# Layer 0's down projection by seven block products from the second chunk on, its right operands prepared in the first

## The chip, the cores and the metric

The kernel runs on one core of one Trainium2 chip. A core has a matrix engine (TensorE, PE in the profile; its weight loads are PEld), three engines for elementwise work (VectorE or DVE, ScalarE or ACT, GpSimd or POOL) and a queue engine (SyncE, SP). Each takes its own instructions strictly in the order in which the built program holds them, and semaphores make one wait for another. DMA transfers are issued by SP, ACT and POOL. The metric is the device time of one execution in microseconds (us), lower is better.

## What is computed

Two layers over 4 sequences of 512 tokens, 512 wide, in float32. Layer 0 adds to its input a recurrent attention and a feed-forward block (FFN), both on the same normed input; layer 1 does the same with latent attention and an expert FFN. The change touches layer 0 alone. Its parts, cut from the reference:

```python
# recurrence of the attention, over 32 mini-batches of K = 16 tokens, 32 heads of 16
def step(carry, x):
    W1_s, b1_s = carry
    xq, xk, xv, eta_mb = x
    Z1 = xk @ W1_s + b1_s
    grad = _ln_fused_l2_bwd(Z1, xv - xk, ln_w, ln_b)
    Attn1 = jnp.tril(xq @ xk.swapaxes(-1, -2))
    b1_bar = b1_s - jnp.tril(eta_mb) @ grad
    Z1_bar = xq @ W1_s - eta_mb * Attn1 @ grad + b1_bar
    last_eta = eta_mb[:, :, -1, :, None]
    W1_new = W1_s - (last_eta * xk).swapaxes(-1, -2) @ grad
    b1_new = b1_s - jnp.sum(last_eta * grad, axis=-2, keepdims=True)
    out = xq + _ln(Z1_bar, ln_w, ln_b)
    return ((W1_new, b1_new), out)

# FFN, 512 -> 1408 -> 512
g = jnp.einsum('th,ih->ti', xf, gate_w) * gate_s
u = jnp.einsum('th,ih->ti', xf, up_w) * up_s
hdn = jax.nn.silu(g) * u
out = jnp.einsum('ti,hi->th', hdn, down_w) * down_s

x = x + _L0_attn_ref(xn, ...) + _L0_ffn_ref(xn, ...)
```

## The kernel before

Layer 0 takes about the first 975 us. Its 2048 tokens are handled in 8 chunks (`NCHUNK`) of 256: 4 sequences of 64 tokens. A chunk holds 4 steps of the recurrence (`CH`), so there are 32 steps (`NM`).

The recurrence is a chain of small operations over several engines. The main loop (L781 to L797) does for each step `n`: `weights_out` copies the state `wacc` into the block-diagonal operand `wq_bd`; `first_product` (PE) forms `pz`; `queries_out` (PE) begins `pso`; `gradient` is some fifteen short operations on DVE and ACT from `pz` to `grad`; `out_operands` builds `gh` on POOL; `update` (L393) copies `grad` into `g_bd` and adds to `wacc` on PE, with `km` from POOL as the other operand; `emit_out` (L434) finishes `pso` on PE from `gh`; `prepare` (L303) fetches the next step's `kv` on POOL's queue and makes `sk` and `km` on POOL.

While the chain runs over DVE, ACT and POOL, PE does other work. That work is a generator, `work` (L698), which chains `between(ch)` over the chunks, and `fill(us)` takes pieces from it until their declared PE times (the numbers that they `yield`) add up to `us`. The tuple `GAPS` (L37) gives the filler between a step's parts: before the update, before the output, after it; `LAST_GAPS` does so for the last chunk's steps. `between(ch)` (L656) consists of: 11 times `gate_up` (two products of 128x256 over 4 blocks each, then SiLU and a product into `hid`), the constants of the end (`finish_constants`, chunk 0 alone), then, interleaved by `take`, the next chunk's transposes, keys, token tiles and queries (`nxt`), `down`, and pieces of `finish(ch - 1)`, which normalises the attention's output, multiplies it by `wo`, adds the FFN's part `yf` and writes the layer's result.

The program is then built by a scheduler that sets each engine's order of instructions itself, from its own estimates of when operands are ready and from the order of the code. So what stands between two of a step's parts on PE in the built program is not what `GAPS` names, only near it.

`down(ch, u)` (L483) computes 128 rows of the FFN's output: for each of 11 blocks `i` of 128 inner columns it loads 256 KB of `in_wd` on SP's queue into a tile `w` (tag `wd`, 4 buffers) and multiplies `hid` by it into `pd`, 512 columns wide. Then DVE multiplies by the row `dsc` (`down_s` spread over all partitions), and POOL adds `brow` (a constant row from the post-norm's bias) and the residual `xr`, which it loads itself.

A tile pool hands out buffers in rotation per tag: a tile asked for under a tag waits until the tile that held its buffer has had its last reader. Loads stand in their queue's order, so one that waits for a buffer holds up those behind it.

Four-byte matmuls are recorded twice each in the profile (a program's matmul of `pd` counts 2 in the table).

Of the kernel before, what the change touches and what calls it, by code (L numbers as in the profile page):

```python
# [12 lines left out]
F32 = mybir.dt.float32  # L13
# [5 lines left out]
P = 128  # L19
B, L, HS = 4, 512, 512  # L20
# [3 lines left out]
NH, HD, K = 32, 16, 16  # L24
# [7 lines left out]
CW = B * CT  # L32
NS = 8
RW = 2 * 64 + 4

START = 20.0
GAPS, LAST_GAPS = (11.0, 3.0, 8.0), (10.0, 3.0, 7.0)  # L37
LAST_FINISH = (10.0, 14.0, 7.0, 0.0, 3.0, 1.0)
TTT_EPS = 1e-6
LN_EPS = 1e-5  # L40
# [2 lines left out]
NI = INTER // P  # L43
# [12 lines left out]
def trunk_kernel(ctx: ExitStack, tc: tile.TileContext, a: dict, out: bass.AP):  # L56
    nc = tc.nc
# [8 lines left out]
    ident = const.tile([P, P], F32, tag="ident", name="ident")  # L66
# [39 lines left out]
    with ExitStack() as px:  # L106
# [9 lines left out]
        def mm(out, lhsT, rhs, start=True, stop=True):  # L116
            nc.tensor.matmul(out, lhsT=lhsT, rhs=rhs, start=start, stop=stop, skip_group_check=True)  # L117

        def psum():
            return ps_pj.tile([P, 512], F32, tag="pj", name="pj")  # L120
# [61 lines left out]
        nc.scalar.dma_start(out=rows_small[:, P:], in_=a["tok"].unsqueeze(0))  # L182
        bones = load(one, "bones", [P, P], eng=nc.scalar)
        m2 = load(one, "m2", [P, 2], eng=nc.scalar)
        gamma_row = wk.tile([P, HS], F32, tag="xr", name="gamma_row")
        gbeta_row = one.tile([P, HS], F32, tag="gbeta_row", name="gbeta_row")
        lrw = load(one, "lrw", [P, NC, P], a["lrw"].rearrange("(c p) m -> p c m", p=P))
        wq_w = load(one, "wq", [P, NC, HS], a["wq"].rearrange("(c p) o -> p c o", p=P))
# [12 lines left out]
        tok = lrb[:, P:]  # L201


        sel8 = one.tile([NS, P], F32, tag="sel8", name="sel8")
        tok8 = one.tile([NS, 2, 4, HD], F32, tag="tok8", name="tok8")
        for h in range(2):
            r = slice(4 * h, 4 * h + 4)
            nc.gpsimd.dma_start(
# [249 lines left out]

        gs = load(one, "gs", [P, NI], eng=nc.gpsimd)
        us = load(one, "us", [P, NI], eng=nc.gpsimd)  # L460
        dsc = one.tile([P, HS], F32, tag="dsc", name="dsc")
        nc.gpsimd.dma_start(out=row["dsc"], in_=a["dsc"].unsqueeze(0))
        hid, yf = {}, {}

# [36 lines left out]
        ch8 = one.tile([NS, 4, 32], F32, tag="ch8", name="ch8")  # L501
# [12 lines left out]

        def finish_constants():
            nc.sync.dma_start(out=wo, in_=a["wo"].rearrange("(c p) o -> p c o", p=P))
            spread_row(dsc, row["dsc"])
            pt = psum()[:, :NS]
            nc.tensor.transpose(pt, ch8.rearrange("s al x -> s (al x)"), ident[:NS, :NS])
            nc.vector.tensor_copy(by_ch, pt)  # L520
            yield 1.0

            pt = psum()[:, :NC]
            mm(pt, onesd, beta_ch)
            beta_m = wk.tile([P, 1], F32, tag="beta_m", name="beta_m", bufs=1)
            nc.vector.tensor_reduce(beta_m, pt, AX.X, ALU.add)
            nc.vector.tensor_scalar(beta_ch, beta_ch, beta_m, None, ALU.subtract)

            pr = psum()
            for c in range(NC):  # L530
                pnb_b = wk.tile([P, P], F32, tag="pnb_b", name=f"pnb_b{c}")
# [190 lines left out]
        pt = psum()[:, :P]  # L722
# [186 lines left out]
    with ExitStack() as px:  # L909
# [623 lines left out]
```

## Time and profile before

| | |
|---|---|
| runs | 1992.97, 1993.64, 1996.19 us; median 1993.64 |
| profiled execution | 1996.04 us, span 1994.3 us |
| mean granted PE clock | 0.994 |
| PE busy | 1938.3 us, 97% |
| DVE, ACT, POOL busy | 1169.6 (59%), 816.1 (41%), 528.2 (26%) us |
| matmuls of the way down, `pd` | 352 records, 166.1 us |
| matmuls of `gate_up`, `pf` | 1408 records, 343.2 us |
| loads of `in_wd` | 176 of 256 KB, 3.1 us from issue to landing |

The span is what the profiler saw of one execution; about 1.7 us of the execution lie around it. "Busy" is the union of an engine's instruction times. Matmuls overlap one another in the pipeline, so the mean time of one record (600 ns for `pd`) is longer than the distance from one to the next.

```profile
PE   8999999999999999998999999999999999999999
DVE  4445748466666657474555656556555655655565
POOL 5333343424333342512000101111211121222223
DMA  6757566646456455745651135444344444333344
```

This is the span in 40 slices of some 50 us, each digit a share of busy time in tenths. Layer 0 fills the first 20: there DVE, POOL and the DMA engines are at work beside PE throughout, and PE has its few gaps.

### The profile page before, as it was taken

How to read it: one execution, taken by the hardware profiler on the slowest of the kernel's cores; microseconds unless marked ns; L12 is line 12 of the kernel's file. 1: busy time of each engine (PE TensorE's matmuls, PEld its weight loads, DVE VectorE, ACT ScalarE, POOL GpSimd, SP SyncE). 2: the span in 40 equal slices, each digit the busy share in tenths (PEclk: the TensorE clock that was granted, in tenths of full speed). 3: DMA queues.
4: the chain of work that ended last, by engine and by line, in shares of the span. 5: the costliest groups of instructions: out<-in, count | busy, mean ns of one | idle time of the engine just before them, and what ended most of it. 6: DMA issues, size and time to landing. Idle time of an engine off the chain costs nothing.

```text
span 1994.3 us, 32414 instructions
## 1 busy us (share of the span) xinstructions
PE 1938.3 (97%) x11626; PEld 1233.3 (62%) x11626; DVE 1169.6 (59%) x2579; ACT 816.1 (41%) x1695; POOL 528.2 (26%) x643
## 2 busy tenths in 40 slices
PE   8999999999999999998999999999999999999999
PEld 6777676767766676753777744555555555555555
DVE  4445748466666657474555656556555655655565
ACT  2234333334433443422222155455545545555552
POOL 5333343424333342512000101111211121222223
PEclk9999999999999999999999999999999999999999
DMA  6757566646456455745651135444344444333344
GB/s 170 210 130 209 143 185 167 175 120 179 141 145 189 126 173 159 224 128 195 225 168 49 58 94 141 118 106 104 101 111 108 103 110 108 95 101 98 89 115 117
DMA packets 226924, 273.51 MB, mean 137 GB/s; under 512 B 88587, under 2 KB 117452, under 8 KB 226124
## 3 DMA queue, kind: packets, MB, share of 16 engines
q1 hardware_dynamic: 204928, 237.19, 43.3%
q0 software_dynamic: 9760, 28.41, 5.0%
q10 hardware_dynamic: 12076, 5.84, 1.0%
q8 instruction: 93, 1.52, 0.3%
q14 instruction: 67, 0.55, 0.1%
HBM read 174.18 MB, written 34.87 MB: 105 GB/s over the span
## 4 chain that ended last, share of the span: by engine, by line
PE 49%; DVE 1%; DMA 0%; ACT 0%; issue 0%; SPq 0%; DVEq 0%; ACTq 0%
PE pc L1254 11%; PE sc L1207 9%; PE pq L1184 8%; PE px L1301 5%; PE p L1301 4%; PE pk L1184 3%; PE epg L976 3%; PE epo L1039 1%; PE epu L976 1%; PE eox L1069 1%; PE pvo L891 1%; PE pw L866 1%; PE eo L1069 1%; DMA gu<-in_gu 0%; DVE st L1225 0%; ACT prob L1227 0%
## 5 line engine op out<-in xcount | busy, mean ns | idle before, releaser
L1225 DVE TENSOR_REDUCE st<-sc 128x1 f32<-128x512 f32 x256 | 168.9, 681 | 244.0 <-PE sc L1207 244.0
L1227 ACT ACTIVATE prob<-sc,st 128x512 f32<-128x512 f32 x256 | 175.1, 686 | 210.5 <-DVE st L1225 210.3
L1254 PE MATMUL pc<-prT,lv 128*128 128x512 f32 x512 | 230.8, 593 | 0.0
L1232 ACT ACTIVATE prob<-prob,st 128x512 f32<-128x512 f32 x256 | 181.9, 720 | 58.8 <-DVE st L1231 58.8
L1236 DVE STREAM_TRANSPOSE tt<-prob 128x512 f32<-128x512 f32 x256 | 178.4, 700 | 43.0 <-ACT prob L1232 36.5
L117 PE MATMUL pf<-xT,wg 128*128 128x256 f32 x704 | 175.6, 391 | 6.2 <-DMA wg<-in_wg 4.4
L1184 PE MATMUL pq<-cq,uq 128*128 128x512 f32 x384 | 175.2, 592 | 0.0
L117 PE MATMUL pf<-xT,wu 128*128 128x256 f32 x704 | 167.6, 381 | 1.5 <-DMA wu<-in_wu 1.5
L117 PE MATMUL pd<-wd,hid 128*128 128x512 f32 x352 | 166.1, 600 | 1.3 <-DMA wd<-in_wd 1.2
L1254 PEld LDWEIGHTS pc<-prT,lv 128*128 128x128 f32 x512 | 96.4, 190 | 100.1 <-issue 98.1
L117 PEld LDWEIGHTS pf<-xT,wg 128*128 128x128 f32 x704 | 133.2, 194 | 33.5 <-issue 4.7
L1207 PE MATMUL sc<-k,q 32*128 32x512 f32 x1024 | 145.7, 617 | 2.5 <-ACT prob L1227 2.5
L117 PEld LDWEIGHTS pf<-xT,wu 128*128 128x128 f32 x704 | 134.5, 191 | 20.5 <-DMA wu<-in_wu 1.9
L478 DVE SCALAR_TENSOR_TENSOR hid<-pf,us,sg 128x256 f32<-128x256 f32 x88 | 42.0, 478 | 156.9 <-ACT sg L477 156.4
L1184 PEld LDWEIGHTS pq<-cq,uq 128*128 128x128 f32 x384 | 74.1, 193 | 90.7 <-issue 90.0
L314 POOL TENSOR_SCALAR sk<-k,m 128x256 f32<-128x256 f32 x64 | 61.2, 968 | 179.9 <-PE pz L117 167.7
L1195 POOL TENSOR_TENSOR kr<-kr,t2k 128x512 f32<-128x512 f32 x16 | 20.3, 1270 | 332.3 <-DVE t2k L1194 332.3
L421 POOL TENSOR_SCALAR gh<-grad,m 128x256 f32<-128x256 f32 x64 | 61.2, 966 | 154.5 <-DVE grad L390 131.6
L117 PEld LDWEIGHTS pd<-wd,hid 128*128 128x128 f32 x352 | 63.4, 190 | 60.2 <-issue 43.8
L1207 PEld LDWEIGHTS sc<-k,q 32*128 32x128 f32 x1024 | 48.4, 185 | 82.7 <-issue 73.2
L477 ACT ACTIVATE sg<-pf,gs 128x256 f32<-128x256 f32 x88 | 41.6, 473 | 132.8 <-PE pf L117 132.3
L1256 ACT COPY ctxT<-pc 128x512 f32<-128x512 f32 x64 | 37.4, 585 | 127.2 <-PE pc L1254 127.1
(316 smaller groups left out, 3467.9 us busy)
## 6 DMA issues: line engine op xcount, KB each, us to landing
prT<-tt SPq DMA_DIRECT2D x992, 64.0 KB, 2.0
wd<-in_wd SPq DMA_DIRECT2D x176, 256.0 KB, 3.1
wg<-in_wg SPq DMA_DIRECT2D x88, 256.0 KB, 3.0
wu<-in_wu SPq DMA_DIRECT2D x88, 256.0 KB, 3.1
cq<-lat_d SPq DMA_DIRECT2D x48, 256.0 KB, 3.8
rows<-rows SPq DMA_DIRECT2D x128, 66.0 KB, 2.2
kv<-rows POOLq DMA_DIRECT2D x32, 264.0 KB, 4.1
gu<-in_gu SPq DMA_DIRECT2D x3, 2048.0 KB
```

What stands on the lines that cost most here:

```text
L117: nc.tensor.matmul(out, lhsT=lhsT, rhs=rhs, start=start, stop=stop, skip_group_check=True)
L314: nc.gpsimd.tensor_scalar_mul(sk[:, :, :, h, :], at(k1[ch], slice(0, P)), m2[:, h : h + 1])
L421: nc.gpsimd.tensor_scalar_mul(gh[:, :, h, :], g, m2[:, h : h + 1])
L976: nc.tensor.matmul(ps, lhsT=w[:, c, :], rhs=x[:, c], start=start and c == 0, stop=c == 1, skip_group_check=True)
L1184: nc.tensor.matmul(ps, lhsT=columns(ws[hg][w]), rhs=x, start=(i == 0), stop=(i == len(srcs) - 1))
L1207: nc.tensor.matmul(ps[h], lhsT=qk[f"q{c}"][r, i * P : (i + 1) * P], rhs=qk[f"k{c}"][r, :], start=(n == 0), stop=(n == 2),)
L1225: pin(nc.vector.tensor_reduce(mx, ps[h], AX.X, ALU.max, negate=True))
L1227: pin(nc.scalar.activation(pr, ps[h], AF.Exp, bias=mx, scale=1.0, accum_out=sm))
L1232: pin(nc.scalar.mul(pr, pr, sm))
L1236: nc.vector.transpose(out=tt[:, :, h - 2], in_=pr.rearrange("p (k kq j) -> p kq k j", kq=4, j=32))
L1254: pin(nc.tensor.matmul(pc, lhsT=lv[:, b, k, :], rhs=at[:, :, k, :], start=(k == 0), stop=(k == E - 1)))
L1301: nc.tensor.matmul(ps[:, q, :], lhsT=a[:, k, q * P : (q + 1) * P], rhs=w[:, k, :], start=start and k == 0 and q == 0, stop=k == 1, skip_gr ...
```

## The change

1. **Seven products.** From chunk 1 on, the way down of a chunk (256 tokens x 1408 by 1408 x 512) is no longer 22 matmuls of 512 columns. The first 1280 inner columns are split in two halves, tokens and output columns in two halves each, and the 2x2 block product is formed from 7 block products instead of 8, in the form with shared sums (Winograd's of Strassen's): left operands `a11`, `a12`, `s1`, `s2`, `a21` (overwritten by a difference), `a12 - s2`, `a22`, right operands 0 to 6. Each block product is 5 matmuls of 256 columns. The last 128 inner columns are done plainly: 4 matmuls of 256 columns (`last`), with a kept tile `last_d`. The partial sums are added into `yf` by DVE, eight adds of 128x256 per chunk.
2. **Right operands.** `down_operands` forms them in chunk 0, one piece at each `gate_up` (`next(rights, None)`), for 5 blocks: a 512 KB load on POOL's queue into the one buffer `hs`, a product with `dsc` on DVE, four differences on DVE, three stores of 128, 256 and 512 KB into `rights_d` in DRAM on POOL's queue. Since `hs` has one buffer, a block's load waits for the stores of the block before. Later chunks read 640 KB per product on SP's queue into two buffers (tag `wd`).
3. **Chunk 0** does its way down plainly (`plain_down`), with two inner blocks per load.
4. **Moved.** `spread_row(dsc, ...)` and the transposition of `ch8` to `by_ch` go from `finish_constants` to the start of `down_operands`. The residual goes straight into `yf`, loaded on SP at `gate_up` 1 (`residual`). The left sums are formed on DVE after `gate_up` 9.
5. **Gaps.** The third numbers of `GAPS` and `LAST_GAPS` go from 8.0 and 7.0 to 7.55 and 6.55. The declared time of the way down goes from 18.86 to 16.84 us per chunk.
6. Small tiles change their places in memory (`gamma_row`, `sel8`, `tok8`, `ch8`, `pnb_b`), so that the new ones fit.

```diff
-GAPS, LAST_GAPS = (11.0, 3.0, 8.0), (10.0, 3.0, 7.0)
+GAPS, LAST_GAPS = (11.0, 3.0, 7.55), (10.0, 3.0, 6.55)
...
-        gamma_row = wk.tile([P, HS], F32, tag="xr", name="gamma_row")
+        gamma_row = wk.tile([P, HS], F32, tag="wg", name="gamma_row")
...
-        def down(ch, u):
-            xr = wk.tile([P, HS], F32, tag="xr", name=f"xr_{ch}_{u}")
-            load_rows(xr, a["x"], ch, u)
-            pd = ps_dn.tile([P, HS], F32, tag="pd", name=f"pd_{ch}_{u}")
-            for i in range(NI):
-                w = wk.tile([P, HS], F32, tag="wd", name=f"wd_{ch}_{u}_{i}", bufs=4)
-                nc.sync.dma_start(out=w, in_=a["wd"][i * P : (i + 1) * P, :])
-                mm(pd, hid[ch][:, i, u * P : (u + 1) * P], w, i == 0, i == NI - 1)
-                if i in (3, 7):
-                    yield 3.43
-            t = wk.tile([P, HS], F32, tag="yf", name=f"yf_{ch}_{u}", bufs=4)
-            nc.vector.tensor_mul(t, pd, dsc)
-            nc.gpsimd.tensor_add(xr, xr, brow)
-            nc.gpsimd.tensor_add(t, t, xr)
-            yf[ch, u] = t
-            yield 2.57
+        KH, half = NI // 2, HS // 2
+        rights_d = dram.tile([7, P, KH, half], F32, tag="rights_d", name="rights_d")
+        scales = {}
+        def down_operands():
+            dsc = scales["down"] = wk.tile([P, HS], F32, tag="yf", name="dsc", bufs=4)
+            spread_row(dsc, row["dsc"])
+            pt = psum()[:, :NS]
+            nc.tensor.transpose(pt, ch8.rearrange("s al x -> s (al x)"), ident[:NS, :NS])
+            nc.vector.tensor_copy(by_ch, pt)
+            nc.gpsimd.dma_start(out=last_d, in_=a["wd"][2 * KH * P :, :])
+            pairs = a["wd"][: 2 * KH * P].rearrange("(k i p) o -> i p k o", k=2, i=KH)
+            for i in range(KH):
+                raw = wk.tile([P, 2, HS], F32, tag="hs", name=f"wd_{i}", bufs=1)
+                nc.gpsimd.dma_start(out=raw, in_=pairs[i])
+                yield
+                nc.vector.tensor_mul(raw, raw, dsc.unsqueeze(1).to_broadcast([P, 2, HS]))
+                b11, b12, b21, b22 = (raw[:, k, o : o + half] for k in range(2) for o in (0, half))
+                t = wk.tile([P, KH, half], F32, tag="wd", name=f"td_{i}")
+                nc.vector.tensor_sub(t[:, 0], b12, b11)
+                nc.vector.tensor_sub(t[:, 1], b22, t[:, 0])
+                nc.vector.tensor_sub(t[:, 2], b22, b12)
+                nc.vector.tensor_sub(t[:, 3], b21, t[:, 1])
+                nc.gpsimd.dma_start(out=rights_d[0][:, i], in_=b11)
+                nc.gpsimd.dma_start(
+                    out=rights_d[1:3, :, i].rearrange("j p o -> p j o"), in_=raw[:, 1].rearrange("p (j o) -> p j o", j=2)
+                )
+                nc.gpsimd.dma_start(out=rights_d[3:, :, i].rearrange("j p o -> p j o"), in_=t[:, :4])
+                yield
+            nc.vector.tensor_mul(last_d, last_d, dsc)
+        rights = down_operands()
+        def residual(ch):
+            for u in range(2):
+                t = yf[ch, u] = wk.tile([P, HS], F32, tag="yf", name=f"yf_{ch}_{u}", bufs=4)
+                load_rows(t, a["x"], ch, u)
+        def left_sums(ch):
+            a11, a12, a21, a22 = (
+                hid[ch][:, k * KH : (k + 1) * KH, u * P : (u + 1) * P] for u in range(2) for k in range(2)
+            )
+            s = wk.tile([P, 2, KH, P], F32, tag="hs", name=f"hs_{ch}", bufs=1)
+            nc.vector.tensor_add(s[:, 0], a21, a22)
+            nc.vector.tensor_sub(s[:, 1], s[:, 0], a11)
+            nc.vector.tensor_sub(a21, a11, a21)
+            left[ch] = dict(a11=a11, a12=a12, a21=a21, a22=a22, s1=s[:, 0], s2=s[:, 1])
+        def plain_down(u):
...
+            for i in range(0, NI, 2):
+                n = min(2, NI - i)
+                w = wk.tile([P, 2, HS], F32, tag="wd", name=f"wd_0_{u}_{i}")[:, :n]
+                nc.sync.dma_start(out=w, in_=a["wd"][i * P : (i + n) * P, :].rearrange("(k p) o -> p k o", p=P))
+                for k in range(n):
+                    mm(pd, hid[0][:, i + k, u * P : (u + 1) * P], w[:, k], i + k == 0, i + k == NI - 1)
...
+        def down(ch):
+            if ch == 0:
+                yield from chain(plain_down(0), plain_down(1))
+                return
...
+            def add(ps, u, oh):
+                t = yf[ch, u][:, oh * half : (oh + 1) * half]
+                nc.vector.tensor_add(t, ps, t)
+            def product(ps, x, j, start, more=None):
+                w = wk.tile([P, KH, half], F32, tag="wd", name=f"wd_{ch}_{j}")
+                nc.sync.dma_start(out=w, in_=rights_d[j])
+                for k in range(KH):
+                    mm(ps, x[:, k, :], w[:, k, :], start and k == 0, k == KH - 1 and more is None)
+                if more:
+                    last(ps, *more, False)
...
+            x = ps_dn.tile([P, HS], F32, tag="pd", name=f"pd_{ch}")[:, :half]
+            product(x, o["a11"], 0, True)
+            for u in range(2):
+                tc.keep_in_program_order(nc.gpsimd.tensor_add(yf[ch, u], yf[ch, u], brow))
+            add(x, 0, 0)
+            yield 2.16
+            p2 = bank("p2")
+            product(p2[:, 0], o["a12"], 1, True, (0, 0))
+            last(p2[:, 1], 1, 1, True)
...
+            product(x, o["s2"], 4, False)
...
+            product(p5, o["s1"], 3, True)
...
+            product(x, o["a21"], 5, False)
...
+            product(p3, o["a12"], 2, True, (0, 1))
...
+            product(x, o["a22"], 6, False, (1, 0))
...
         def finish_constants():
             nc.sync.dma_start(out=wo, in_=a["wo"].rearrange("(c p) o -> p c o", p=P))
-            spread_row(dsc, row["dsc"])
-            pt = psum()[:, :NS]
-            nc.tensor.transpose(pt, ch8.rearrange("s al x -> s (al x)"), ident[:NS, :NS])
-            nc.vector.tensor_copy(by_ch, pt)
-            yield 1.0
...
                 if i == NI - 3:
                     yield from take(fin, 1)
+                if ch == 0:
+                    next(rights, None)
+                if i == 1:
+                    residual(ch)
+                if i == NI - 2 and ch:
+                    left_sums(ch)
...
-            for u in range(2):
-                dn = down(ch, u)
-                for j in range(3):
-                    yield from take(nxt, 2)
-                    yield from take(dn, 1)
-                    yield from take(fin, 1)
+            dn = down(ch)
+            for j in range(7):
+                yield from take(nxt, 2)
+                yield from take(dn, 1)
+                yield from take(fin, 1)
```

More of the change, by code (lines that the diff above doesn't have):

```diff
@@ L201, in trunk_kernel @@
         tok = lrb[:, P:]
-        sel8 = one.tile([NS, P], F32, tag="sel8", name="sel8")
-        tok8 = one.tile([NS, 2, 4, HD], F32, tag="tok8", name="tok8")
+        eights = wk.tile([P, 3, P], F32, tag="gh", name="eights")[:NS]
+        sel8, ch8 = eights[:, 0], eights[:, 2].rearrange("s (al x) -> s al x", al=4)
+        tok8 = eights[:, 1].rearrange("s (j al d) -> s j al d", j=2, al=4)
         for h in range(2):
@@ L460, in trunk_kernel @@
         us = load(one, "us", [P, NI], eng=nc.gpsimd)
-        dsc = one.tile([P, HS], F32, tag="dsc", name="dsc")
+        last_d = one.tile([P, HS], F32, tag="last_d", name="last_d")
         nc.gpsimd.dma_start(out=row["dsc"], in_=a["dsc"].unsqueeze(0))
@@ L501, in trunk_kernel @@
-        ch8 = one.tile([NS, 4, 32], F32, tag="ch8", name="ch8")
+        KH, half = NI // 2, HS // 2
[27 more added lines that the diff above has]
+            nc.vector.tensor_mul(last_d, last_d, dsc)
@@ new lines, in trunk_kernel @@
+        rights = down_operands()
+        left = {}
+        def residual(ch):
[11 more added lines that the diff above has]
+            left[ch] = dict(a11=a11, a12=a12, a21=a21, a22=a22, s1=s[:, 0], s2=s[:, 1])
@@ new lines, in plain_down @@
+        def plain_down(u):
+            pd = ps_dn.tile([P, HS], F32, tag="pd", name=f"pd_0_{u}")
+            for i in range(0, NI, 2):
[4 more added lines that the diff above has]
+                    mm(pd, hid[0][:, i + k, u * P : (u + 1) * P], w[:, k], i + k == 0, i + k == NI - 1)
+                if i in (2, 6):
+                    yield 3.43
+            t, s = yf[0, u], wk.tile([P, HS], F32, tag="xt", name=f"ys_{u}", bufs=4)
+            nc.vector.tensor_mul(s, pd, scales["down"])
+            nc.gpsimd.tensor_add(t, t, brow)
+            nc.gpsimd.tensor_add(t, t, s)
+            yield 2.57
@@ new lines, in down, with last, bank @@
+        def down(ch):
+            if ch == 0:
+                yield from chain(plain_down(0), plain_down(1))
+                return
+            o = left.pop(ch)
+            def add(ps, u, oh):
[8 more added lines that the diff above has]
+                    last(ps, *more, False)
+            def last(ps, u, oh, start):
+                mm(ps, hid[ch][:, NI - 1, u * P : (u + 1) * P], last_d[:, oh * half : (oh + 1) * half], start, True)
+            def bank(nm):
+                return ps_ff.tile([P, 2, CW], F32, tag="pf", name=f"{nm}_{ch}")
+            x = ps_dn.tile([P, HS], F32, tag="pd", name=f"pd_{ch}")[:, :half]
[7 more added lines that the diff above has]
+            last(p2[:, 1], 1, 1, True)
+            add(p2[:, 0], 0, 0)
+            add(p2[:, 1], 1, 1)
+            yield 3.02
+            product(x, o["s2"], 4, False)
+            add(x, 0, 1)
+            nc.vector.tensor_sub(o["a12"], o["a12"], o["s2"])
+            yield 2.16
+            p5 = bank("p5")[:, 0]
+            product(p5, o["s1"], 3, True)
+            add(p5, 0, 1)
+            add(p5, 1, 1)
+            yield 2.16
+            product(x, o["a21"], 5, False)
+            add(x, 1, 1)
+            yield 2.16
+            p3 = bank("p3")[:, 0]
+            product(p3, o["a12"], 2, True, (0, 1))
+            add(p3, 0, 1)
+            yield 2.59
+            product(x, o["a22"], 6, False, (1, 0))
+            add(x, 1, 0)
+            yield 2.59
@@ L530, in finish_constants @@
             for c in range(NC):
-                pnb_b = wk.tile([P, P], F32, tag="pnb_b", name=f"pnb_b{c}")
+                pnb_b = wk.tile([P, CW], F32, tag="sg", name=f"pnb_b{c}")[:, :P]
                 nc.vector.tensor_copy(pnb_b, pnb[:, c : c + 1].to_broadcast([P, P]))
```

## The prediction

> **What bounds the kernel now.** I read the page's busy table first, then the waits of PE, then the timelines of PE, POOL and DVE around the first recurrence steps, and last the order of the instructions on each engine in both built programs (an order holds no times).
>
> ```profile
> PE 1938.3 (97%) x11626; PEld 1233.3 (62%) x11626; DVE 1169.6 (59%) x2579; ACT 816.1 (41%) x1695; POOL 528.2 (26%) x643
> ...
> L117 PE MATMUL pd<-wd,hid 128*128 128x512 f32 x352 | 166.1, 600 | 1.3 <-DMA wd<-in_wd 1.2
> ```
>
> PE is busy for 1938.3 of 1994.3 us, so 56 us are idle in all. A PE matmul that is taken out is time won, if PE has something else to do at once; a wait put into PE's order is time lost in full. The way down (`pd`) costs two records per matmul of 512 columns, 352 in all, and waits for almost nothing.
>
> ```profile
> PE pj L117 <- ACT pn_sq L549: 6.9, 3, 3.1
> PE pso L117 <- POOL gh L421: 5.8, 4, 2.7
> PE pf L117 <- DMA wg<-in_wg: 4.4, 2, 2.2
> PE wacc L117 <- DVE g_bd L395: 3.7, 3, 1.7
> ...
> PE pj L117 <- DVE by_ch L520: 2.4, 1, 2.4
> ```
>
> These are PE's longest waits; those on `gh` and `g_bd` are the recurrence showing through, 9.5 us in 32 steps. The chain from `pz` over the gradient to `wacc` is hidden by other matmuls in nearly all of the 32 steps.
>
> **What is taken out.** Eight back-to-back records of 256 columns take 1.73 us (`pf` 59.58 to 61.31), 0.216 each. A program matmul is two records, so 0.43 us at 256 columns; the `pd` groups give 0.86 at 512. A chunk's way down was 22 x 0.864 = 19.0 us. It becomes 7 products x 5 matmuls, and 4 for the last rows, 39 x 0.432 = 16.85. Seven chunks save 7 x 2.16 = **15.1 us**. Chunk 0 keeps 22. Gaps shortened by 0.45 us in 32 steps ask for 14.4 us less filler, so the filler per step keeps its measure. Two POOL adds of 1.26 us per chunk go too, off the path.
>
> **What is added, off PE.** GpSimd's queue gets 21 DMAs in chunk 0 (the last rows; five times a 512 KB load and stores of 128, 256 and 512 KB). An issue there costs 0.57 us (kv at 56.41), 12 us on an engine that is 26% busy. DVE gets five times a 128x1024 product (half of 2.29 for 128x2048 at 12.47, so 1.15) and four 128x256 differences at 0.42, 14.2 us; then some 5 us more per later chunk (left sums, eight adds at 0.42, less two of 0.69). By amount this fits. By place it doesn't: POOL and DVE run in order, and at step 0 these stand inside the gradient's chain.
>
> **Step 0.** Three timelines, of PE, DVE and POOL; columns are start, duration, engine, line, operation, and in brackets the idle time before and what ended it.
>
> ```profile
> 46.40 1.08 PE L117 MATMUL pz<-wq_bd,sk 128*32 128x128 f32 x32
> 47.30 0.63 PE L117 MATMUL pso<-wq_bd,wh 128*32 128x64 f32 x32
> ...
> 51.38 0.59 PE L117 MATMUL pj<-by_ch,onesd 128*128 128x4 f32 x2 [2.39 <-DVE by_ch L520]
> 51.83 3.76 PE L117 MATMUL pf<-xT,wg 128*128 128x256 f32 x8
> ...
> 82.42 0.65 PE L117 MATMUL wacc<-g_bd,km 128*32 128x64 f32 x32
> ```
>
> ```profile
> 58.09 0.90 DVE L395 COPY g_bd<-grad 32x256 f32<-32x256 f32 x2
> ```
>
> ```profile
> 57.03 2.20 POOL L321 TENSOR_SCALAR km<-kv,m2n 128x256 f32<-128x256 f32 x2
> 59.19 0.57 POOL L307 DMA_DIRECT2D kv<-rows  x1
> 59.81 1.82 POOL L421 TENSOR_SCALAR gh<-grad,m 128x256 f32<-128x256 f32 x2
> ```
>
> The reader sees `pz` end at 47.3, `g_bd` ready at 59.0 and `gh` at 61.6, while PE does `pf` matmuls until 82.4: 28.5 us of filler. In the changed order there is none. After `pz`, `pso` and the small `beta_m` product PE's next instruction is `wacc`, then `pso<-gh`, and `pf_2` to `pf_8` stand behind both. The latency of 11.7 us from `pz` to `g_bd` lies bare. On DVE it loses the copies of `dsc` and `by_ch` (0.85, moved ahead) and gains the product and four differences of block 1 (1.15 + 1.68 = 2.8), so 13.7. About 0.9 of it is covered by `pso` and `beta_m`: 12.8 idle at least. Then `gh` (0.8 + 1.8 after `g_bd`) leaves another 1 to 2 behind `wacc` (0.65).
>
> It is worse if transfers are slow. Block 1's load waits in POOL's order for the stores of block 0; step 0's `kv` load and `km` stand behind such loads. Rows of POOL's queue: kv 264 KB 4.1 us, z 128 KB 3.7, zb 512 KB 5.4. With 4.2 and 3.0 (about the fastest rows) the updates start at 61.7, with 5.4 and 4 at 64.6 or later. The Trainium skill ("DMA: Bandwidth & Descriptors", "Anatomy of one DMA — SWDGE (gpsimd) path") puts a transfer of GpSimd's queue at 2.0 us and its bytes at 436 GB/s, 3.2 us for 512 KB. The row of zb says 5.4; by the page's figure the blocks would never be late and the stall would be the lower end.
>
> Against the 2.4 idle here before, the step costs +11 to +16. Later blocks make DVE wait in order for loads 3 and 4 ahead of the `hid` copies, which hold `pf`'s two buffers: +1 to +7. I take **+13** for the whole of chunk 0's start, near the fast rows, as the blocks are plain 2 KB rows; ends +11 and +22.
>
> **Step 3.** PE's order before had 10.4 us of filler between `pz` and `wacc`, now 3.5, and none from `wacc` to the next `pz` (10.4 before). PE's and POOL's timelines there:
>
> ```profile
> 145.05 0.63 PE L117 MATMUL pso<-wq_bd,wh 128*32 128x64 f32 x32
> ...
> 156.17 0.65 PE L117 MATMUL wacc<-g_bd,km 128*32 128x64 f32 x32
> 159.06 3.54 PE L117 MATMUL pf<-xT,wg 128*128 128x256 f32 x8 [2.23 <-DMA wg<-in_wg]
> ```
>
> ```profile
> 154.71 1.83 POOL L421 TENSOR_SCALAR gh<-grad,m 128x256 f32<-128x256 f32 x2
> ```
>
> `gh` ended at 156.5 and one `pf` block (3.46) ends at 149.1: 7.4 idle, and then 1.3 for the `wq_bd` copies (at 265.0 to 267.3, a step without filler, PE lost 2.3 less 1.0 of `pz`). Taken off: the 2.23 wait at 159.06 and about 1 of clock behind it. **+6**, ends +3 and +8. Step 2 (10.2 to 7.6 of filler against a chain of 9.8): **+1.6**.
>
> **Steps 4 to 31.** Filler before and after, against a chain of some 9.8 us to `g_bd` and 11.6 to `gh`: worse at 14, 22 (emission after 8.3 instead of 12.1), 26 (8.6), 28 (7.8) and 31 (8.6), in sum 6.4; better at 7 (7.3 to 8.6) and 24 (6.9 to 9.5), 2.8. **+3.6**, ends 0 and +8. DVE's additions at steps 17 and 21 lengthen the chain by up to 3.8 us, under a filler of 14 to 17 us: nothing; it would be 3.8 each without.
>
> **Weights of the products.** 640 KB each, on SP, in two buffers: a load starts when the product two before it ends. Landing is estimated at 4.3 us, between 256 KB (3.1) and 1024 KB (`wo` 5.3). Where PE has less than that between (0.9 to 3.0 us in chunks 2, 3, 4 and 7) the third product waits 1 to 3.5 us. At 4.3 that sums to 7 (1.3 each in chunks 2 and 3, 3.5 in 4, 1 and more in 6 and 7), at 3.1 to 1. **+4**, between the two; ends 0 and +10 (landing as wo's). Before, `wd` cost 1.2. Chunk 0's own loads are 512 KB in two buffers instead of 256 KB in four, as many bytes ahead as before: nothing, up to 2 if they land as zb does. SP's residual loads wait for `yf` buffers ahead of a `wg` load in chunk 1; by the order that load is in time.
>
> **The clock.**
>
> ```profile
> 50.00:55.00 5.00, 3.62 (x10) 2.99 (x11) 3.21 (x12) 0.48 (x2) 2.73 (x6) 0.51 0.35 110
> ```
>
> This windows row ends with the granted clock, 0.51, after the idle 2.39 at step 0. The windows in which it fell (50 to 57, 160 to 164, 266 to 273, 925 to 928, 1160 to 1164) hold some 24 us at half clock, about 12 lost, 3.4 of it here. A stall of 13 costs one such ramp as well as one of 2.4, so the term cancels at step 0; one more at step 3 and one fewer at step 7: **0**, ends -3 and +6. The Trainium skill ("TensorE: Matmul & The Clock Gate", "Part 1: The HAM clock gate (the "warmup" mystery)") has the clock halved only after an idle window of about 3.4 us; here 2.4 sufficed. By the page's rule the short stalls would be free of ramps and the two new long ones not, some 3 us more.
>
> **Sum.** -15.1 + 13 + 6 + 1.6 + 3.6 + 4 + 0 = +13.1 on a span of 1994.3 in an execution of 1996.04 (1.7 around the span, which the change leaves alone): 2009 for such an execution. The median shown, 1993.64, is 2.4 under it; +13 on the median gives **2007**. All low ends: -15.1 + 11 + 3 + 1 + 0 + 0 - 3 = -3, so 1990; all high ends: -15.1 + 22 + 8 + 2 + 8 + 10 + 6 = +41, 2034, which would need all at once; the range stops at 2028. Below it reaches to 1984, into the first rival.
>
> **Rivals.**
> A: the change does what it is made for: the saving of 15.1 stays and stalls hardly cost, because idle falls elsewhere (step 7, the `pn_sq` waits) as it rises here. It needs step 0's chain to be short, and PE's order speaks against it: the 11.7 us are fixed by DVE's own rows. With no stall at all 1979; with half of the low ends of steps 0 and 3 (+7 of 14) 1986. For it: before, 56 us of idle leave room to win. 20%.
> B: balance, stalls at the low ends, 1990 to 1998, mid 1994, no change. 10%.
> C, one mechanism beyond mine on the slow side: DVE stands at block loads in order. If a POOL store and load take 10 us a round rather than 7, all `hid` copies, and so `pf`, wait behind each of five blocks; +15 over mine, 2022. It decides from landings above 5 us. zb's 5.4 speaks for it, kv's 4.1 against. 20%.
> D: the forecast, 50%, own range 1998 to 2016.
>
> A measurement here tells 0.2%, 4 us, from no change. Faster: A and a little of B; same: most of B; slower: C and D. The range leaves out the lower half of A and the far end of C.
>
> **What would show it.** PE's wait list with a `wacc` wait at step 0 of 12 us or more, a `pso<-gh` wait of some 7 in step 3, `pd`/`pf` waits for the new weights summing to 4, layer 0's PE busy down by 15. I am wrong if `wacc` at step 0 comes within 8 us of `pz`, or if idle falls elsewhere by as much as it rises there.

## The result, and the profile after

The changed kernel takes 2039.19 us (median of 4 runs, 2037.74 to 2043.72) against 1994.69 of the kernel before on the same chip: a ratio of 1.0227, interval 1.0208 to 1.0246. The forecast of 2007 had the direction and not the size; 2039 lies above the range's end of 2028. The profiled execution has a span of 2036.0 us, 41.7 more than the 1994.3 before.

From the page after, the busy table and the DMA issues:

```profile
PE 1937.6 (95%) x11864; PEld 1286.6 (63%) x11864; DVE 1215.1 (60%) x2682; ACT 823.3 (40%) x1700; POOL 530.2 (26%) x650
...
wd<-rights_d SPq DMA_DIRECT2D x49, 640.0 KB, 4.4
```

PE is idle for 2036.0 - 1937.6 = 98.4 us, 42.4 more than before. And it is busy for as long as before (-0.7), although some 15 us of matmuls were taken out. So there are two losses: new idle time, and matmuls that ran more slowly. The granted clock's mean fell from 0.994 to 0.984.

PE's waits after (total, number, longest):

```profile
PE wacc L117 <- DVE g_bd L396: 19.3, 4, 15.1
PE pso L117 <- POOL gh L422: 16.6, 5, 7.9
PE pj L117 <- ACT pn_sq L648: 6.5, 2, 3.6
PE pj L117 <- DVE pn_sq L641: 6.1, 4, 2.7
PE pf L117 <- DVE hid L479: 5.1, 2, 4.4
...
PE p L117 <- DVE hid L479: 3.6, 1, 3.6
...
PE p L117 <- DMA wd<-rights_d: 3.0, 2, 2.8
```

The waits for `g_bd` and `gh`, the recurrence, were 9.5 us together and are 35.9. Summing the gaps in PE's timeline from one `pz` to the next gives the places: 21.3 us idle in step 0 (2.8 before), 0.8 in step 2 (0), 7.9 in step 3 (2.2), 43.0 in steps 4 to 30 (27.5). The rest of the span, step 31 with it, has 1.9 more.

Step 0 on PE, DVE and SP after (start, duration, engine, line, operation; in brackets the idle time and what ended it):

```profile
49.39 0.39 PE L117 MATMUL pj<-by_ch,onesd 128*128 128x4 f32 x2
64.91 1.08 PE L117 MATMUL wacc<-g_bd,km 128*32 128x64 f32 x32 [15.14 <-DVE g_bd L396]
...
67.17 3.38 PE L117 MATMUL pf<-xT,wg 128*128 128x256 f32 x8
...
83.58 3.68 PE L117 MATMUL pf<-xT,wg 128*128 128x256 f32 x8 [4.41 <-DVE hid L479]
```

```profile
52.92 0.52 DVE L369 TENSOR_TENSOR xh<-xh,r 128x256 f32<-128x256 f32 x1
56.07 1.23 DVE L501 TENSOR_TENSOR wd<-wd,dsc 128x1024 f32<-128x1024 f32 x1 [2.64 <-DMA wd<-in_wd]
...
81.91 1.22 DVE L501 TENSOR_TENSOR wd<-wd,dsc 128x1024 f32<-128x1024 f32 x1 [7.27 <-DMA wd<-in_wd]
83.05 0.48 DVE L479 SCALAR_TENSOR_TENSOR hid<-pf,us,sg 128x256 f32<-128x256 f32 x1
```

```profile
36.85 2.41 SPq L127 DMA_DIRECT2D yf<-in_x  x4
39.79 0.36 SPq L472 DMA_DIRECT2D wg<-in_wg  x1
```

PE stands 15.1 us at `wacc`, with only `pso` and the small `beta_m` product between `pz` and it, as the built order said. On DVE the first wait for a block's load (2.64) and the block's product stand inside the gradient's chain; the second shown (7.27) holds a `hid` copy, and with it `pf`. SP issues the residual's loads ahead of that of `wg`.

After these stalls PE comes back slowly. Windows of after: stretch, its length, busy time of PE, PEld, DVE, ACT and POOL, granted clock, DMA share, GB/s:

```profile
64.00:68.00 4.00, 2.96 (x60) 2.48 (x61) 3.89 (x8) 0.00 (x0) 4.00 (x4) 0.50 0.14 56
84.00:88.00 4.00, 4.00 (x13) 3.21 (x13) 1.35 (x4) 0.00 (x0) 2.22 (x4) 0.62 0.62 220
...
674.00:678.00 4.00, 3.67 (x68) 2.64 (x69) 3.92 (x8) 0.00 (x0) 3.20 (x4) 0.57 0.02 4
```

These follow waits of 15.1, 4.4 and 5.5 us; the granted clock is 0.50 to 0.62. `pf` with eight records shows it too: 3.68 at 83.58, 1.89 at full clock.

### The profile page after: what moved, and what is told of

It reads as the page before. It is cut to its first block, busy times and chain, and to the rows that moved or that the text cites. A ratio compares the mean times of both kernels' runs of the same rounds, so it can differ in the third digit from the quotient of the medians.

```text
span 2036.0 us, 32830 instructions
## 1 busy us (share of the span) xinstructions
PE 1937.6 (95%) x11864; PEld 1286.6 (63%) x11864; DVE 1215.1 (60%) x2682; ACT 823.3 (40%) x1700; POOL 530.2 (26%) x650
## 5 line engine op out<-in xcount | busy, mean ns | idle before, releaser
L1299 POOL TENSOR_TENSOR kr<-kr,t2k 128x512 f32<-128x512 f32 x16 | 20.3, 1271 | 330.4 <-DVE t2k L1298 330.4
L1378 POOL TENSOR_TENSOR t_ops<-vo 128x512 f32<-128x512 f32 x4 | 5.2, 1288 | 286.5 <-PE eo L1173 201.0
L317 POOL COPY wq_bd<-q 32x256 f32<-32x256 f32 x128 | 55.4, 433 | 81.0 <-PE pso L117 51.0
```

## The experiments

Each is one edit or a few away from a kernel named with it. Ratios are to the kernel before, on the same chip, with their intervals.

**1. What took step 0's filler: the residual's loads.** In the changed kernel, as built, `pf_2` and all that follows stood behind `wacc`. First, the loads of the residual later (`res_late_all`):

```diff
-                if i == 1:
+                if i == 8:
                     residual(ch)
```

> One line differs from the changed kernel: the residual's four loads stand on SP behind gate_up 8 of each chunk instead of gate_up 1. In the built order step 0 has 28 us of filler again, and step 3 has 17 us behind its update. Theory P (the prediction's: the preparation's work on DVE and POOL is what costs the first chunk): little is won, 2030 to 2037, and PE still waits over 8 us at step 0's wacc. Theory R (the residual's loads, waiting for yf buffers on SP ahead of the wg loads, took the filler out of PE's order at steps 0 and 3): the 15.1 us at step 0 and the 7.9 us at step 3 go, and a clock ramp with them: 2010 to 2020.

2035.84 us, 1.0208 [1.0191, 1.0225]. The built order has all of step 0's filler back, and the time hardly moves. PE, then DVE of this run:

```profile
55.36 1.89 PE L117 MATMUL pf<-xT,wu 128*128 128x256 f32 x8
71.21 3.78 PE L117 MATMUL pf<-xT,wg 128*128 128x256 f32 x8 [13.96 <-DVE hid L479]
...
84.55 3.78 PE L117 MATMUL pf<-xT,wg 128*128 128x256 f32 x8 [3.27 <-DVE hid L479]
```

```profile
57.59 1.23 DVE L501 TENSOR_TENSOR wd<-wd,dsc 128x1024 f32<-128x1024 f32 x1 [3.99 <-DMA wd<-in_wd]
...
70.68 0.86 DVE L479 SCALAR_TENSOR_TENSOR hid<-pf,us,sg 128x256 f32<-128x256 f32 x2
...
81.29 1.22 DVE L501 TENSOR_TENSOR wd<-wd,dsc 128x1024 f32<-128x1024 f32 x1 [9.74 <-DMA wd<-in_wd]
```

Two `pf` pairs run in the gap, then both buffers are full: the `hid` copies that free them stand on DVE behind the gradient and the block loads. The wait at `wacc` is gone, and waits for `hid` of 17.2 us in all take its place. The block loads, the prediction's rival C, are only a part of them: experiment 3 has the same order on PE with no block loaded, and still waits 6.4 us there. By difference the blocks make some 10.9. And the wait for `gh` in step 3, expected to go with the late residual, stays (7.86).

**2. The products without the preparation, and the preparation without the products.** `products_alone` reads its right operands from plain rows of `wd` and drops the loop over the blocks, so its output isn't the reference's:

```diff
-                nc.sync.dma_start(out=w, in_=rights_d[j])
+                nc.sync.dma_start(out=w, in_=some_rights(j))
```

> The preparation is left out: no block loads, products, differences or stores; the seven products read rows of the down weights in place of the right operands, as many bytes, so the way down's values are not the reference's. The order on PE is that of the changed kernel in every step. Theory P: step 0 loses only the bare chain, and what the preparation added is gone, 2008 to 2016. Theory R: the wait at step 0 shrinks from 15 to some 11 or 12, the wait at hid (4.4) goes, step 3 stays: 2027 to 2034.

2023.98 us, 1.0142 [1.0126, 1.0158]. PE at step 0 of this run:

```profile
49.70 0.39 PE L117 MATMUL pj<-by_ch,onesd 128*128 128x4 f32 x2
63.27 0.32 PE L117 MATMUL pso<-a_bd,gh 128*32 128x68 f32 x1 [13.19 <-POOL gh L422]
```

There is again no filler ahead of the update and the output, and PE stands there for 13.19 us, though nothing is prepared. So the preparation did not take the filler of step 0 away; the residual's loads did. The preparation adds 2.0 us to that wait (15.14), and the `hid` wait of 4.4, which this run doesn't have.

`prep_alone` keeps the preparation, and goes down plainly in all chunks:

```diff
-            if ch == 0:
-                yield from chain(plain_down(0), plain_down(1))
-                return
+            yield from chain(plain_down(ch, 0), plain_down(ch, 1))
+            return
...
-                if i == NI - 2 and ch:
-                    left_sums(ch)
```

> The right operands are prepared as in the change, but every chunk does its way down plainly with 22 matmuls of 512 columns, and no left sums are formed; the new gaps and the early residual stay. It pays 15.1 us more on PE than the change. Theory P: the first chunk's costs of some 20 us in full, 2012 to 2020. Theory D (the later chunks' extra work on DVE, left sums and adds inside the gradient's chain at steps 17 to 30, is worth some 30 us of stall): those stalls are absent, so that it ends 5 to 20 us under the changed kernel though it multiplies more: 2018 to 2034. If later chunks were hardly touched by DVE's work, it would end 10 to 15 above the changed kernel, 2050.

2050.97 us, 1.0277 [1.0252, 1.0301], slower than the whole change. It got an order of its own, with stalls at steps 8, 12, 16, 20, 24 and 28, so it doesn't price the preparation. That it ends at the expectation's 2050 says nothing for the reason given there. Inconclusive.

**3. The residual late and no preparation** (`late_noprep`: the edits of `res_late_all` and `products_alone` together):

> Both edits together: the residual's loads behind gate_up 8, and no preparation (the products read rows of the down weights, so the way down's values are not the reference's). Theory S (two causes in series at step 0, each hidden by the other: without the preparation PE's order still lacks the filler, with the filler DVE still waits for the blocks ahead of the hid copies): the idle time of steps 0 to 3 falls to some 5 us as before, 2003 to 2013. Theory P alone (the preparation, as left out before): no better than 2024. Theory R alone: no better than 2036 less what the preparation costs in issue, 2030.

2017.83 us, 1.0106 [1.0073, 1.0139], 21 us under the changed kernel. By medians the late residual alone gave 3 and the missing preparation alone 15; together they give a little more, as each alone leaves the other's stall in step 0. But the idle time of steps 0 to 3 falls only to 17.2 us (30.0 in the changed kernel, 5.0 before), not to the 5 expected. Two waits make most of it:

```profile
63.02 3.78 PE L117 MATMUL pf<-xT,wg 128*128 128x256 f32 x8 [6.37 <-DVE hid L479]
...
162.91 0.32 PE L117 MATMUL pso<-a_bd,gh 128*32 128x68 f32 x1 [7.78 <-POOL gh L422]
```

The first stands where `res_late_all` waits 13.96: DVE's order has the two `hid` copies behind the whole gradient, with no block load between. The second is step 3's. It is there with the residual late (7.86), without the preparation (7.77) and with both edits (7.78), so these two don't account for it.

**4. The left sums** (`late_noprep_nosums`: as 3, and the products take parts of `hid` as they are, so the sums are left out of what is computed):

```diff
-            nc.vector.tensor_add(s[:, 0], a21, a22)
-            nc.vector.tensor_sub(s[:, 1], s[:, 0], a11)
-            nc.vector.tensor_sub(a21, a11, a21)
...
-            nc.vector.tensor_sub(o["a12"], o["a12"], o["s2"])
```

> As late_noprep, and the four sums of left blocks per chunk (three on DVE before the way down, one within it) are left out; products take plain blocks in their place, so the values are again not the reference's. PE's order is nearly the same. Theory D (these 128x640 operations stand inside the gradient's chain on DVE and ahead of the last hid copy, and cost steps 17, 21, 22, 25, 26 and 28 their stalls): 10 to 20 us under late_noprep, 1988 to 1998. Theory O (PE's order of filler alone sets the stalls): within 4 us of late_noprep.

2011.12 us, 1.0080 [1.0049, 1.0110]; the intervals of 3 and 4 overlap, and the gain by medians, 6.7 us, is under the 10 to 20 expected. Step 21's wait for `gh` falls from 5.53 to 1.40. But PE's waits for `gh` and `g_bd` together are 20.3 us, against 20.6 in 3: others grew by as much.

**5. The gaps.** The changed kernel with the old gaps (`gaps_old`), and the kernel before with the new ones (`before_gaps_new`):

```diff
-GAPS, LAST_GAPS = (11.0, 3.0, 7.55), (10.0, 3.0, 6.55)
+GAPS, LAST_GAPS = (11.0, 3.0, 8.0), (10.0, 3.0, 7.0)
```

> The changed kernel with the gaps of before (8.0 and 7.0). Theory G (the shortened gaps took the filler from the later steps): the waits at gh and g_bd in steps 17 to 30 go, 2015 to 2025. Otherwise only the places of the stalls move, 2032 to 2046.

> The kernel before, with the change's gaps (7.55 and 6.55) and nothing else. Theory G (the gaps were tuned to the work, so any shift lays chains bare): 5 to 15 us slower than before, 2000 to 2010. If the gaps do nothing by themselves: within 4 us, 1990 to 1998.

2040.71 us, 1.0235 [1.0211, 1.0259]: nothing, the stalls only moved. And 2007.19 us, 1.0051 [1.0032, 1.0071]: the gaps alone, with no matmul taken out, cost the kernel before 10 us by another order.

**6. The preparation repaired** (`prep_pinned`). To `res_late_all` it adds: all five blocks are loaded at once, into tiles that lie idle in chunk 0; their products are pinned in program order behind steps 0, 1 and 2, after the gradient's chain.

```diff
-                raw = wk.tile([P, 2, HS], F32, tag="hs", name=f"wd_{i}", bufs=1)
+            for i, (tag, bufs) in enumerate((("hs", 1), ("zb", 1), ("pn_sq", 1), ("q1", 3), ("xT", 3))):
+                raw = wk.tile([P, 2, HS], F32, tag=tag, name=f"wd_{i}", bufs=bufs)
...
+                tc.keep_in_program_order(nc.vector.tensor_mul(raw, raw, dsc.unsqueeze(1).to_broadcast([P, 2, HS])))
...
+            for _ in range((2, 2, 1)[n] if n < 3 else 0):
+                next(rights, None)
```

> The whole change, computed in full, but all five blocks are loaded at once at the start into five tiles that lie idle then, the block products on DVE are held to their place in program order behind steps 0, 1 and 2, and the residual is loaded behind gate_up 8. In the built order steps 0 to 3 have 28, 12, 10 and 10 us of filler ahead of the update, as before the change. Theory S: the first chunk's stalls go, and what is left are the later ones: 2002 to 2014. If the preparation costs by its amount of DMA and DVE work and not by its place: 2020 or more.

2027.51 us, 1.0159 [1.0130, 1.0189]. Steps 0 to 4 have 16.3 us of idle in place of 30.0 (5.9 before). The largest wait that is left in them, from PE's timeline of this run:

```profile
62.99 3.78 PE L117 MATMUL pf<-xT,wg 128*128 128x256 f32 x8 [6.17 <-DVE hid L479]
```

It is the wait that `late_noprep` has there (6.37): no block load is left in it. Step 3's wait for `gh` is gone (0.6 us of idle). The time is still above the 2002 to 2014 expected; steps 4 to 30 have 48.2 us of idle, 43.0 in the changed kernel.

**7. The reciprocals of the finish.** At step 21, PE, DVE and POOL of the changed kernel:

```profile
666.47 2.32 PE L117 MATMUL p<-wd,hid 128*128 128x256 f32 x10
674.33 1.13 PE L117 MATMUL pso<-a_bd,gh 128*32 128x68 f32 x32 [5.54 <-POOL gh L422]
```

```profile
654.40 0.42 DVE L357 TENSOR_REDUCE s<-pz 128x16 f32<-128x256 f32 x1 [0.48 <-PE pz L117]
...
663.88 0.82 DVE L529 TENSOR_TENSOR hs<-hid 128x640 f32<-128x640 f32 x1
...
668.21 1.74 DVE L657 RECIPROCAL pn_rs<-pn_rs 128x256 f32<-128x256 f32 x1
669.88 0.36 DVE L391 TENSOR_TENSOR grad<-u,rl 128x256 f32<-128x256 f32 x1
...
670.54 0.82 DVE L530 TENSOR_TENSOR hs<-hs,hid 128x640 f32<-128x640 f32 x1
671.28 1.42 DVE L661 TENSOR_TENSOR zb<-zb,q 128x1024 f32<-128x1024 f32 x1
672.62 0.81 DVE L531 TENSOR_TENSOR hid<-hid 128x640 f32<-128x640 f32 x1
```

```profile
670.41 3.87 POOL L422 TENSOR_SCALAR gh<-grad,m 128x256 f32<-128x256 f32 x2 [12.48 <-DVE grad L391]
```

The same step before, PE and DVE:

```profile
643.41 0.68 PE L117 MATMUL pso<-a_bd,gh 128*32 128x68 f32 x32 [1.25 <-POOL gh L421]
```

```profile
627.62 0.42 DVE L356 TENSOR_REDUCE s<-pz 128x16 f32<-128x256 f32 x1 [0.48 <-PE pz L117]
...
640.95 0.42 DVE L390 TENSOR_TENSOR grad<-u,rl 128x256 f32<-128x256 f32 x1
```

From the first reduction to the gradient's end DVE takes 15.8 us: four of the finish's reciprocals, 1.75 each, and a left sum lie in it. Before it was 13.7 at the same step (627.62 to 641.37), with three reciprocals and no sum. `gh` takes 3.87 in place of 1.82. That is 2.1 + 2.05 later, and the wait grew from 1.25 to 5.54, under a filler of 14.0 us against 14.2. So the finish's first piece was put behind `gate_up` 4 instead of 8, in three kernels: the repaired one (`pin_fin7`), the changed one (`after_fin7`) and the one before (`before_fin7`).

```diff
-                if i == NI - 3:
+                if i == NI - 7:
                     yield from take(fin, 1)
```

> As prep_pinned, and one number more: the first piece of finish(ch - 1), with its four 128x256 reciprocals (1.75 us each) and products on DVE, is taken behind gate_up 4 instead of gate_up 8, so that it no longer stands in the same step's gradient as the left sums. Theory D2 (reciprocals and left sums together stretch the gradient past its filler at steps 17 and 21): the 5.5 us of gh at step 21 and the late hid copy at step 17 go, 8 to 16 under prep_pinned, 2011 to 2020. Theory O (the order of filler alone): the stalls move to other steps, within 5 us of prep_pinned.

> The changed kernel with that one number. Theory D2: the stalls at steps 17, 21, 22 and 26 go, 12 to 23 us under the changed kernel's 2039, 2016 to 2027, with the first chunk's stalls of 20 us left as they are. If the gain of pin_fin7 came from the first chunk's repair and this edit together: under 8 us.

> The kernel before, with the one number of pin_fin7: the first piece of finish(ch - 1) behind gate_up 4 instead of gate_up 8. It has no left sums. Theory D2 as put (reciprocals hurt only together with the left sums): within 4 us of before. Theory F (the reciprocals in a gradient's chain cost in the kernel before as well): 4 to 10 us faster than before, 1986 to 1992, and part of pin_fin7's gain is none of the change's.

`pin_fin7` 2004.46 us (10 runs), 1.0037 [1.0021, 1.0053]; `after_fin7` 2023.27, 1.0138 [1.0113, 1.0164]; `before_fin7` 1993.81, 0.9993 [0.9978, 1.0007]. The edit is worth 23 us in the repaired kernel, 16 in the changed one, and nothing in the one before: the reciprocals hurt only together with what the change added. The idle time of steps 4 to 30 falls from 43.0 to 31.5 us in the changed kernel and from 48.2 to 29.2 in the repaired one (27.5 before). The edit moves other work in the built order too, so beyond step 21, shown next, that it is the reciprocals is the likely reading and not a shown one. Step 21 of `after_fin7` on PE, DVE and POOL:

```profile
673.34 0.68 PE L117 MATMUL pso<-a_bd,gh 128*32 128x68 f32 x32
```

```profile
659.42 0.42 DVE L357 TENSOR_REDUCE s<-pz 128x16 f32<-128x256 f32 x1
...
669.37 0.42 DVE L391 TENSOR_TENSOR grad<-u,rl 128x256 f32<-128x256 f32 x1
```

```profile
669.96 2.34 POOL L422 TENSOR_SCALAR gh<-grad,m 128x256 f32<-128x256 f32 x2 [7.09 <-DVE grad L391]
```

The reciprocals are done before `pz`, the chain is 10.4 us, and the wait of 5.54 is gone. From the page of `pin_fin7`, and its longest waits of PE:

```profile
PE 1923.4 (96%) x11864; PEld 1277.8 (64%) x11864; DVE 1209.5 (61%) x2682; ACT 825.4 (41%) x1702; POOL 526.4 (26%) x650
```

```profile
PE pj L117 <- ACT pn_sq L651: 12.2, 5, 3.6
PE pf L117 <- DVE hid L479: 11.6, 5, 6.0
```

This execution took 1996.34 us, the shortest of its ten; the others took 2001.6 to 2009.3. It does the same 11864 matmul records as the changed kernel in 14.2 us less of PE's busy time, at a mean clock of 0.995.

**8. From there.** None of these gained on `pin_fin7`:

`noprep_fin7` (as 3, with the finish's piece early) asks what the repaired preparation still costs.

> late_noprep with finish's first piece behind gate_up 4; no preparation, and the products read rows of the down weights in place of the right operands, so the way down's values are not the reference's. If the repaired preparation is hidden: as pin_fin7, 2000 to 2006. If it still costs by its amount: 6 to 14 under pin_fin7, 1990 to 1998, which is also the bound for any place of it.

2006.23 us, 1.0038 [1.0023, 1.0052]: the same as `pin_fin7`. That doesn't show the repaired preparation to be hidden: this run still has step 3's wait for `gh` (7.25), and `pin_fin7` has 0.6 us of idle there, so the two differ in more than the preparation.

`pin_fin7_320` (blocks 3 and 2 behind steps 0 and 1).

> pin_fin7 with the five blocks prepared behind steps 0 and 1 (three and two) instead of 0, 1 and 2, so that no prepared tile shares the wd buffers with the first chunk's own loads in step 2. If those shared buffers make the 2.9 us wait at pd in step 2: 2 to 5 under pin_fin7. Otherwise the same within 3.

2006.59 us, 1.0051 [1.0032, 1.0071].

`combo` (gaps 11.5, 3.0 and 7.05, and two of the last rows' matmuls moved to later products).

> pin_fin7 with two edits more, computed in full: the four matmuls of the last 128 inner columns, which need the last hid copy, are moved from the second product to the fourth and sixth (one DVE add of 128x256 more), and the gaps are 11.5, 3.0 and 7.05. By PE's built order the filler ahead of the update is under 10 us in five steps after the fourth. Theory D2 with the last hid copy as a cause of its own (3.6 us at step 17): 3 to 8 under pin_fin7, 2004 to 2016. If the waits for the products' weights are what is left, no gain over pin_fin7.

2005.89 us, 1.0044 [1.0025, 1.0063].

`pin_fin7_g8` (gaps 8.0 and 7.0).

> pin_fin7 with the gaps of before (8.0 and 7.0). If the shortened gaps are what is left (alone in the kernel before they cost some 10 us): 5 to 12 under pin_fin7, 1992 to 1999. If they only move the stalls: within 5 of it, 1999 to 2009.

2025.87 us, 1.0143 [1.0123, 1.0163]: 21 us, with the same 11864 matmul records.

No version beat the kernel before.

## Why the direction was right and the size was not

Three terms of the sum were too small, the clock's most of all, then that of steps 4 to 31, then step 0's; the others held within 2 us. Against the two profiled spans, in us:

| term | predicted | measured |
|---|---|---|
| matmuls taken out | -15.1 | -14.9, by `pin_fin7`'s busy time |
| chunk 0's start (step 0) | +13 | +18.5 idle |
| step 2 | +1.6 | +0.8 idle |
| step 3 | +6 | +5.7 idle |
| weights of the products | +4 | +3.0 idle (3.9 for `rights_d`, 0.9 for `wd` before) |
| other waits from step 4 on | +3.6 (to step 31) | +12.5 idle (to step 30) |
| clock | 0 | +14.2 |
| outside | 0 | +1.9 idle |
| sum | +13.1 | +41.7 |

The clock's row is the difference of PE's busy time between the changed kernel and `pin_fin7`, which have the same 11864 matmul records; the first row, from one execution of `pin_fin7`, depends on it. Of the 14.2 us, 14.6 lie before one and the same place at the end of layer 0 (890.5 us busy up to 975.47 in the changed kernel, 875.9 up to 928.29 in `pin_fin7`), where the mean clock is 0.97 against 0.99, and -0.4 behind it. A second estimate is PE's busy time weighted with the missing share of the clock, in windows of 4 us up to there: 20.6 us in the changed kernel, 7.5 in `pin_fin7`, 8.9 in the kernel before (up to 934). It puts the term at 11.7 to 13.1.

**What held.** The saving, the lay-bare chain at step 0 (12.8 at least, measured 15.1), the wait for `gh` in step 3 (7.4, measured 7.9), the landing of the products' weights (4.3, measured 4.4) and what they cost. The chain's place was read from the built order, and it was there.

**Step 0, +13.** The lower end was taken, and `wacc` alone used it up. The `hid` wait of 4.4 behind the block loads was named (+1 to +7) but given no full share. The prediction didn't say why the filler had gone; read beside the preparation, it looked like its effect. `products_alone` has no filler there without any preparation, and `res_late_all` has it back: it was the residual's loads, moved ahead on SP. Rival C's mechanism was real. It showed with 4.4 us here, and with some 10.9 of the 17.2 in `res_late_all`. Step 3 was priced rightly, but what took its filler is not known: it is missing with and without the residual's early loads and the preparation, and back in `prep_pinned`. (The filler of step 0 before, put at 28.5 us, is 30.6 by the rows shown, 51.83 to 82.42; nothing hangs on it.)

**Steps 4 to 31, +3.6.** The step that failed is "DVE's additions at steps 17 and 21 lengthen the chain by up to 3.8 us, under a filler of 14 to 17 us: nothing". The filler was set against a chain of 11.6. Step 21's own chain was 15.7 before, by the finish's reciprocals (627.62 to the end of `gh` at 643.36), and there was a wait of 1.25 already: there was no cover. Then every microsecond on DVE and POOL is paid, and POOL's `gh` slowed down by 2.05 besides. `late_noprep_nosums` and `after_fin7` take the two sides of it away, the sums and the reciprocals, and the wait of 5.5 falls to 1.4 and to nothing. With the reciprocals moved, the idle time of steps 4 to 30, the products' weights with it, is 4.0 us above that of before, in place of 15.5.

**The clock, 0.** It was argued that a long stall costs one ramp as a short one does, and that one ramp more and one fewer cancel. At step 0 the first half held: by the estimate above PE lost 2.8 us after the wait of 2.39 before, and 2.5 after that of 15.1. The count failed. In those windows layer 0 has ten stretches with the clock below full, where it had four: twice in step 0, in steps 3, 17, 21, 22 and 28, twice in step 30, and in 31; before in steps 0, 3, 7 and 31. `pin_fin7` has five. In these PE works at a lower clock, beyond its idle time, and the term is nearly as large as the whole saving.

**What stays open.** `pin_fin7` saves the 14.9 us of matmuls and has 71.2 us of idle (56.0 before), so the gain is spent: on `pn_sq`, on `hid`, and in most of its runs on some 8 us more that the profiled one does not show. Which of the products' demands does it was not settled. Why a gap 0.45 us longer costs 21 us there and nothing in the changed kernel was measured, not explained. Why the residual's loads move `wacc` ahead of `pf_2` in the built order is shown as a fact of that order; the rule behind it was not looked for. What takes the filler of step 3, and what puts the `hid` copies of step 0 behind the gradient (6.4 us without any preparation), stays open too.

## What to carry to other kernels

Set each addition against the chain of its own step, with everything that already lies in it; a step that shows even a small wait has no cover left. Price a new stall as its idle time plus matmuls that may run at half clock after it, and count the stalls. When the built order loses its filler, undo each moved load by itself before blaming the largest new work, and expect the next wait in line to take over.

## What the runs showed of the hardware

POOL's `gh` pair took 1.82 us at step 21 before and 3.87 in the changed kernel, 2.05 more, while DVE ran three operations with two inputs from SBUF, where the tiles lie: 0.82 us at 670.54, 1.42 at 671.28 (1.22 for that shape at 81.91) and 0.81 at 672.62. In `after_fin7` it took 2.34, with one such operation of 0.82 us at 669.71, of which 0.57 fell in its time. The Trainium skill ("SBUF — State Buffer", "Who interferes with whom") says that a DVE instruction with two SBUF inputs contends with a GpSimd instruction that reads SBUF, because its second input comes through the shared read interface. These rows agree with it; no run here tried it by itself.

PE's clock fell to half after waits of 4.4 and 5.5 us, as the windows show, and PE was busy 14.2 us longer for the same records. But not every wait did it. One of 3.63 us ended at 853.12 in the changed kernel and one of 3.63 at 816.41 in `pin_fin7`, both at `pj` for `pn_sq`. The windows in which PE went on, of the changed kernel and of `pin_fin7`:

```profile
852.00:856.00 4.00, 2.88 (x5) 1.67 (x6) 3.74 (x10) 1.75 (x3) 4.00 (x5) 0.50 0.46 153
```

```profile
816.00:820.00 4.00, 3.59 (x15) 2.81 (x16) 3.71 (x8) 1.04 (x2) 3.55 (x5) 1.00 0.28 93
```

The granted clock was 0.50 after the first and 1.00 after the second; the length of a wait alone does not tell. The same matmul records in another order (`pin_fin7` and `pin_fin7_g8`) differ by 21 us, more than the change set out to save.
